# Holding a softmax's subtraction and exponential to their own step in the order of VectorE and ScalarE

## The chip, the cores and the metric

The kernel runs on one core of a Trainium2 chip. The metric is the device time of one execution in microseconds (us). PE is TensorE's matmul, PEld its weight load, DVE is VectorE, ACT is ScalarE, POOL is GpSimd and SP is the engine that issues most DMAs.

## The reference, cut to what matters

Two layers run over 1024 latent rows (16 batches of 64, width 128). Each layer attends from the latents to a context of 1601 rows and to the latents themselves, then goes through a scan and a feed-forward block. The attention takes nearly all of the time:

```python
q = ln @ Wq                                  # 16 heads of 64
k, v = split(concat([xn, ln]) @ Wkv)         # xn: normalized context
logits = einsum('bhld,bhsd->bhls', q * scale, k * scale)
w = softmax(logits)                          # layer 1: some context rows are masked
out = einsum('bhls,bhsd->bhld', w, v) @ Wo
x = x + out
x = x + scan_block(layernorm(x))             # after the attention, in each layer
x = x + ffn_block(layernorm(x))              # layer 0: experts; layer 1: 4-bit weights
```

## The kernel before, in words

The key weights are folded into the query and the value weights into the output, so that scores are made straight from the normalized context (`kvT`) and the averages are taken of the context itself (`kv`). A *group* is one layer, one batch and one half of the heads: 8 heads by 64 latents, or 512 columns. There are 64 groups. The context of a group is cut into 13 tiles of 128 rows, so a group has 13 *steps* and the whole has 832.

`step(n, ng)` writes the work of step n. The pieces that it calls belong to different groups, because the softmax has to know a group's maximum before it can weigh anything:

- `scores(g, i)`, L534: two matmul passes (L547) make a score tile `s` of 128x512 in PSUM, from a pool `pss` of three buffers. ACT copies it into the SBUF tile `st` (the "evict": L554 in layer 0, L552 in layer 1, where the mask is added). DVE takes the running maximum `R` (L561 or L559) from the same score tile. Two score tiles make a pair, one `st` tile of 128x1024; the thirteenth stands alone. A group has seven pairs, j = 0 to 6.
- `maximum(g)`, L564, one step after the group's last scores: transposes `tm` of R on PE and a reduction on DVE give the maximum `m`.
- `spread`, L584, two steps later: four matmuls (L588) write the maximum, spread over partitions, into a PSUM tile `mb`. It comes from the pool `pst` (tag `tp`) of three buffers that nearly all other small matmuls share, and lives until the group's last subtraction.
- `weigh(g, j)`, L591: DVE subtracts `mb` from the pair in place (L596), ACT takes the exponential in place (L597). It is written at the steps o = 3, 5, ..., 15 after the group's scores have ended.
- `average(g, i)`, L599, 21 steps behind the scores (`LAG`): matmuls (L609) with `st` as weights add the weighted context into a PSUM tile `av`, of which there is one (`psa`, two banks).
- `gather(g)`, L611: DVE takes the four parts out of `av` (L618) before the next group's averages can start.

Two further lists of generators are run beside the steps: `prep` (context, queries, latents of coming groups) and `between` (scans, experts, feed-forward blocks).

The order in which instructions stand on an engine is not the order of writing. A scheduler in the framework orders them by its own estimate of times, by the order of writing among those that are ready, and by any added edge. The kernel adds such edges with `behind(back)`, L1301. For the instructions that were written inside the block it looks up, for each engine, an instruction of the main pipeline in the list `self.place` (the score matmuls for PE, the evicts for ACT, the maxima for DVE), and lets none of them stand ahead of it. On PE this is always the latest score matmul; on ACT and DVE it is the latest for `back=0` and the one before it for `back=1`. The edge has no semaphore: it sets the order in the queue, and no wait at run time.

```python
for e, k in (("PE", 0), ("ACT", back), ("DVE", back)):
    if len(self.place[e]) > k:
        i = self.place[e][-1 - k]
        where[i.engine] = i
```

Of what is written in the steps, all but the scores, the averages, the gather and the weighing is already inside such a block.

Of the kernel before, what the change touches and what calls it, by code (L numbers as in the profile page):

```python
# [77 lines left out]
class Kernel:  # L78
# [1239 lines left out]
    def step(self, n, ng):  # L1318
        g, i = divmod(n, NT)
        if g < ng:  # L1320
            self.scores(g, i)

        ga, ia = divmod(n - LAG, NT)
        if 0 <= ga < ng and ia:
            if ia == 1:
                self.average(ga, 0)
            self.average(ga, ia)
            if ia == NT - 1:
                self.gather(ga)

        for p in (g - 2, g - 1):
            o = n - (p + 1) * NT
            if not 0 <= p < ng:
                continue
            if o == 1:
                with self.behind():
                    self.maximum(p)
            elif o == 3:
                with self.behind():
                    self.groups[p]["mb"] = self.spread(self.groups[p]["m"], f"mb{p}")  # L1340
            if o > 2 and o % 2 and (o - 3) // 2 < (NT + 1) // 2:
                self.weigh(p, (o - 3) // 2)

        d, o = divmod(n - LAG - NT, NT)
        if 0 <= d < ng:
            lay, b, half = self.groups[d]["key"]
            last = d == ng - 1
            with self.behind():
                if o == 0:
                    self.denominator(d)  # L1350
                elif o == (1 if last else 4):
                    self.turn(d)
                if last:
                    if o == 1:
                        self.output(lay, b // 2, 1)
                elif o == 7 and b % 2 and half:
                    self.output(lay, b // 2)
                elif o == 9 and d == ng - 2:
                    self.output(lay, b // 2, 0)
# [57 lines left out]
```

## Time and profile before

| | us |
|---|---|
| median of 3 runs | 2039.4 (2036.52 to 2041.78) |
| the profiled execution | 2037.05 |
| its span, first to last instruction | 2035.3 |
| PE busy | 1959.3 |
| PEld busy | 1486.4 |
| DVE busy | 1558.3 |
| ACT busy | 1405.2 |
| POOL busy | 512.0 |

The table is of one execution with the profiler. Engines run beside one another, so the busy times don't add up to the span. A matmul's end is modelled, and neighbouring matmuls overlap in the trace, so PE's busy time can hide short stalls. Where a row of the profile ends in an arrow, the engine sat idle before that work until the named work was done.

### The profile page before, as it was taken

The numbers are of one execution on the slowest core, as the hardware profiler recorded it, in microseconds if no ns is written. First come the engines' busy times: TensorE is split into PE (matmuls) and PEld (weight loads), VectorE is DVE, ScalarE is ACT, GpSimd is POOL, SyncE is SP. The second block draws the span as 40 slices with busy tenths as digits, with TensorE's granted clock in tenths as the row PEclk, the third lists the DMA queues.
The fourth block names the chain that finished last, engine by engine and source line by source line (L and its number), as shares of the span: only waits on it lengthen the run. The fifth ranks groups of instructions, "written<-read, shape, count | busy, mean of one in ns | idle before, by whom it ended". The sixth has DMA issues, their size and how long they took to land. (4 is left out here: it accounts for less than half of the span.)

```text
span 2035.3 us, 32662 instructions
## 1 busy us (share of the span) xinstructions
PE 1959.3 (96%) x12005; PEld 1486.4 (73%) x12005; DVE 1558.3 (77%) x2893; ACT 1405.2 (69%) x2673; POOL 512.0 (25%) x581
## 2 busy tenths in 40 slices
PE   7999999999999999999999999999999999999994
PEld 5677777676777766778777787777778777787783
DVE  4886667987777897776988777898686878778774
ACT  5787878888668887666767657776566656675651
POOL 3112113543113452121443203442111121101000
PEclk9999999999999999999999999999999999999996
DMA  5211112221122222221221102221120111101000
GB/s 143 69 60 52 52 52 73 82 66 50 35 76 86 66 76 57 64 74 47 67 80 50 36 24 71 75 59 51 43 56 15 57 36 47 46 1 36 23 1 21
DMA packets 142956, 110.53 MB, mean 54 GB/s; under 512 B 11458, under 2 KB 129486, under 8 KB 142798
## 3 DMA queue, kind: packets, MB, share of 16 engines
q1 hardware_dynamic: 140598, 107.40, 18.1%
q8 instruction: 95, 1.56, 0.3%
q10 hardware_dynamic: 2200, 1.06, 0.3%
q14 instruction: 63, 0.52, 0.1%
HBM read 79.97 MB, written 27.41 MB: 53 GB/s over the span
## 5 line engine op out<-in xcount | busy, mean ns | idle before, releaser
L609 PEld LDWEIGHTS av<-kv,st 128*128 128x128 f32 x6656 | 849.3, 192 | 310.1 <-issue 282.6
L609 PE MATMUL av<-kv,st 128*128 128x129 f32 x6656 | 866.1, 276 | 4.5 <-DVE aq L618 3.1
L547 PE MATMUL s<-qT,kvT 128*128 128x512 f32 x1664 | 848.5, 600 | 17.2 <-DVE R L561 14.5
L596 DVE TENSOR_TENSOR st<-st,mb 128x1024 f32<-128x1024 f32 (+1 forms) x448 | 502.5, 1135 | 1.2 <-PE mb L588 1.1
L597 ACT ACTIVATE st<-st 128x1024 f32<-128x1024 f32 (+1 forms) x448 | 445.5, 998 | 63.1 <-DVE st L596 59.5
L552 ACT ACTIVATE st<-s,mcol 128x512 f32<-128x512 f32 x416 | 283.8, 685 | 222.8 <-PE s L547 177.4
L554 ACT COPY st<-s 128x512 f32<-128x512 f32 x416 | 240.9, 583 | 125.9 <-PE s L547 99.0
L547 PEld LDWEIGHTS s<-qT,kvT 128*128 128x128 f32 x1664 | 258.9, 191 | 91.0 <-DVE R L561 40.2
L559 DVE SCALAR_TENSOR_TENSOR R<-s,mcol,R 128x512 f32<-128x512 f32 x352 | 262.9, 747 | 70.6 <-ACT st L552 69.6
L561 DVE TENSOR_TENSOR R<-s,R 128x512 f32<-128x512 f32 x352 | 241.6, 686 | 81.4 <-ACT st L554 79.6
L483 POOL TENSOR_TENSOR kv<-kv,vec 128x384 f32<-128x384 f32 (+1 forms) x128 | 135.9, 1081 | 155.4 <-PE kt L521 65.0
L628 POOL TENSOR_TENSOR aq<-aq,rd 128x512 f32<-128x512 f32 x63 | 77.0, 1222 | 359.2 <-DVE rd L625 351.9
L730 POOL TENSOR_TENSOR db<-sc_u,bb 128x512 f32<-128x512 f32 x64 | 84.8, 1327 | 134.8 <-DVE h L741 64.8
L747 POOL TENSOR_TENSOR sc_y<-sc_y,h 128x512 f32<-128x512 f32 x60 | 80.0, 1334 | 105.3 <-DVE h L746 81.3
L513 ACT ACTIVATE kv<-kv,coff,crstd 128x128 f32<-128x128 f32 x195 | 82.1, 494 | 8.2 <-POOL coff L510 8.2
L741 DVE TENSOR_TENSOR_SCAN h<-da,db 128x512 f32<-128x512 f32 x64 | 85.3, 1333 | 0.0
L504 ACT ACTIVATE scr<-kv,cmean 128x128 f32<-128x128 f32 x195 | 78.8, 404 | 6.9 <-DVE cmean L500 3.6
L561 DVE TENSOR_TENSOR R<-s,st 128x512 f32<-128x512 f32 x32 | 22.1, 690 | 78.4 <-ACT st L554 78.4
L618 DVE SCALAR_TENSOR_TENSOR aq<-xeb,ee,av 128x129 f32<-128x129 f32 x256 | 74.3, 346 | 3.4 <-PE av L609 3.4
L117 POOL TENSOR_TENSOR crstd<-cvar,neghalf 128x13 f32<-128x13 f32 x15 | 37.5, 2497 | 145.7 <-DVE cvar L508 145.5
L416 PE MATMUL q<-xnT,wqk 128*128 128x128 f32 x512 | 69.8, 281 | 0.0
L416 PEld LDWEIGHTS q<-xnT,wqk 128*128 128x128 f32 x512 | 64.4, 196 | 6.8 <-issue 3.3
(369 smaller groups left out, 1942.8 us busy)
## 6 DMA issues: line engine op xcount, KB each, us to landing
bb<-bcd SPq DMA_DIRECT2D x64, 256.0 KB, 4.4
xh<-kv SPq DMA_DIRECT2D x16, 832.0 KB, 4.8
kv<-xh SPq DMA_DIRECT2D x16, 832.0 KB, 5.4
kvT<-xhT SPq DMA_DIRECT2D x16, 800.0 KB, 4.5
xhT<-kvT SPq DMA_DIRECT2D x15, 800.0 KB, 3.5
kv<-in_ctx_dram SPq DMA_DIRECT2D x15, 768.0 KB, 5.2
ew<-in_e1T_dram SPq DMA_DIRECT2D x36, 64.0 KB, 1.8
ew<-in_e3T_dram SPq DMA_DIRECT2D x36, 64.0 KB, 1.9
```

Source lines behind the costliest of these rows:

```text
L416: nc.tensor.matmul(t[:, k * P:(k + 1) * P], self.wqk[:, g * 4 + k, :], xnT, start=True, stop=True)
L483: nc.gpsimd.tensor_tensor(kv[:, lo:hi, :D], kv[:, lo:hi, :D], self.row(self.vec[:, w1, :], [P, hi - lo, D]), ALU.mult)
L547: mm = nc.tensor.matmul(s, self.kv_of[lay, b][1][:, i * P:(i + 1) * P], q, start=True, stop=True)
L552: ev = nc.scalar.activation(st, s, AF.Identity, bias=mc)
L554: ev = nc.scalar.copy(st, s)
L559: mx = nc.vector.scalar_tensor_tensor(R, s, mc, last, ALU.add, ALU.max)
L561: mx = nc.vector.tensor_tensor(R, s, last, ALU.max)
L596: nc.vector.tensor_tensor(st, st, self.row(mb, [P, n, NQ]), ALU.subtract)
L597: nc.scalar.activation(st, st, AF.Exp)
L609: nc.tensor.matmul(o, st, self.kv_of[lay, b][0][:, i, :], start=(i == 0 and k % 2 == 0), stop=(i == NT - 1 and k % 2 == 1))
L730: nc.gpsimd.tensor_tensor(db, u, self.row(bb[:, 0, s % 2, :], both), ALU.mult)
L741: nc.vector.tensor_tensor_scan(flat(h), flat(da), flat(db), 0.0, ALU.mult, ALU.add)
```

## The change

The call of `weigh` in `step` is put into a block `behind(1)`. The subtraction of a pair may then not stand ahead of the last but one maximum written so far on DVE, nor its exponential ahead of the last but one evict on ACT. Nothing else is changed: same instructions, same buffers, same sizes. The edges act on the framework's ordering as a whole, so other instructions can change places too.

```diff
@@ -1339,7 +1339,8 @@
                 with self.behind():
                     self.groups[p]["mb"] = self.spread(self.groups[p]["m"], f"mb{p}")
             if o > 2 and o % 2 and (o - 3) // 2 < (NT + 1) // 2:
-                self.weigh(p, (o - 3) // 2)
+                with self.behind(1):
+                    self.weigh(p, (o - 3) // 2)
 
         d, o = divmod(n - LAG - NT, NT)
         if 0 <= d < ng:
```

## The prediction

> **What bounds the kernel now.** I read the page first, then the stages, then the waits, then one stretch in order of time. The page:
>
> ```profile
> span 2035.3 us, 32662 instructions
> PE 1959.3 (96%) x12005; PEld 1486.4 (73%) x12005; DVE 1558.3 (77%) x2893; ACT 1405.2 (69%) x2673; POOL 512.0 (25%) x581
> L596 DVE TENSOR_TENSOR st<-st,mb 128x1024 f32<-128x1024 f32 (+1 forms) x448 | 502.5, 1135 | 1.2 <-PE mb L588 1.1
> L597 ACT ACTIVATE st<-st 128x1024 f32<-128x1024 f32 (+1 forms) x448 | 445.5, 998 | 63.1 <-DVE st L596 59.5
> ```
>
> TensorE (PE) is the bound. The two rows below it are the work that the change holds: 448 subtractions on DVE and 448 exponentials on ACT. Each pair is 2.3 us of work, and a step of the pipeline (one score tile) lasts (1956-30)/832 = 2.31 us, from the first and last start of the score matmuls. The stages:
>
> ```profile
> 60.00:1960.00 1900.00, 1870.20 (x11505) 1416.73 (x11504) 1492.02 (x2710) 1352.03 (x2545) 483.82 (x516) 1.00 0.18 53
> 1960.00:2036.00 76.00, 44.02 (x296) 38.11 (x294) 38.73 (x102) 18.35 (x33) 5.49 (x12) 0.77 0.05 15
> ```
>
> The first column after the length is PE busy: idle 29.8 us in the body, 32 us in the tail. A change that moves only DVE and ACT work inside the body can win those 29.8 us, plus stalls that sit inside PE's modelled busy time, and no more. What PE waits for (us in total, times, longest):
>
> ```profile
> PEld s L547 <- DVE R L561: 40.2, 44, 2.5
> PEld s L547 <- DVE R L559: 18.4, 28, 1.5
> PE s L547 <- DVE R L561: 14.5, 17, 1.7
> PE s L547 <- DVE R L559: 2.2, 4, 0.7
> PEld av L609 <- ACT st L597: 6.1, 11, 2.4
> ```
>
> The score matmul waits for the running maximum R on DVE: R is the last reader of a score tile in PSUM, and there are three such buffers, so s of step i+3 waits for R of step i. The average's wait for the exponential is small. One stretch shows why R is late:
>
> ```profile
> 998.96 2.34 DVE L596 TENSOR_TENSOR st<-st,mb 128x1024 f32<-128x1024 f32 x2
> 1001.22 0.74 DVE L559 SCALAR_TENSOR_TENSOR R<-s,mcol,R 128x512 f32<-128x512 f32 x1
> 1001.88 1.21 DVE L596 TENSOR_TENSOR st<-st,mb 128x1024 f32<-128x1024 f32 x1
> ...
> 1004.26 1.21 DVE L596 TENSOR_TENSOR st<-st,mb 128x1024 f32<-128x1024 f32 x1
> 1005.39 0.75 DVE L559 SCALAR_TENSOR_TENSOR R<-s,mcol,R 128x512 f32<-128x512 f32 x1
> ...
> 1006.19 0.30 PEld L547 LDWEIGHTS s<-qT,kvT 128*128 128x128 f32 x2 [0.70 <-DVE R L559]
> 1007.11 0.30 PEld L547 LDWEIGHTS s<-qT,kvT 128*128 128x128 f32 x2 [0.62 <-DVE R L559]
> ```
>
> Four subtractions of a group come nearly together, DVE has no idle time from 1000 to 1012 (12.00 busy of 12.00), R falls behind, and three scores that PE runs back to back (while the previous group's sums are taken out of PSUM) find no free buffer.
>
> [...]
>
> **The change, part by part.** It adds no instruction and takes none away; the sum of busy times stays. It adds order only: the subtraction and exponential of pair j, at step o = 3+2j after their group's scores, must follow the maximum and the copy out of PSUM (evict) of the step before. I compared the built order of both programs. "Ahead of R_7" means the seventh maximum of the following group.
>
> - Subtractions: the median pair stood after R_3, 3, 4, 5, 8, 9, 10 (j = 0 to 6); now after R_3, 4, 6, 8, 10, 11, 14. Ahead of R_6 stood 3.52 per group, now 1.97; ahead of R_7 4.31, now 2.79. That is 1.5 x 1.21 = 1.85 us less DVE work in front of just those maxima that the back-to-back scores s_9 and s_10 wait for. Two or more subtractions between neighbouring maxima: 79 places, now 1.
> - Exponentials: ahead of evict 7 stood 2.97 per group, now 1.97: 1.06 us less ACT work ahead of it, and R waits for the evict.
> - What it is worth. The exposed s-waits: the PE rows are stall in full (14.5 + 2.2 = 16.7 us). Of the PEld rows most is hidden, because a weight load has a running matmul to hide behind: in the stretch, two waits of 1.32 us cost PE 0.19 us (three scores took 1008.07 - 1005.29 = 2.78 us; one takes 0.86, as from 1000.04 to 1000.90 where nothing waits, so 2.59 unhindered). At that share 58.6 us are 8 us. Sum 25 us. Were all of them gone: -25. The waits are 0.8 us each (58.6+16.7 over 93), below the 1.85 us that is taken out, but DVE also works on scans (1.22 and 0.68 us) and the taking-out (4 x 0.35), so that it stays behind in part. I take 60%: -15 us. Ends: 0 and -25.
> - What is late next. The subtractions go to steps 8 to 14, where DVE had about 1.5 fewer. Worked out from the starts and ends in the trace, the room between R of step i and s of step i+3 is, in the median, 3.3 us or more for i = 9 to 12, against 1.0 and 0.5 us for i = 6 and 7. A subtraction of 1.21 us fits. Some of the later R will slip; I take +2 us, between 0 and +8 (10 of 62 groups at 0.8 us).
> - Exponential before average: the median time from exponential to the average that reads it is between 10 and 17 us for each j. The exponentials move later by 0 to 3 steps in the median, at most 7 us; 3 us or more stay in the median, so no wait is added as a rule. The average's order on PE hardly moves (3154 of 3328 matmuls stand between the same scores, 152 earlier, 22 later). Cost 0, up to +6 (a doubling of the 6.1 us).
> - ACT: an exponential now stands closer to its subtraction, and what is queued behind it is the next evict. "ACT st <- DVE st" is 59.5 us in 88 waits now, 0.68 each; ACT is 69% busy. I take +1, between 0 and +10.
> - SP and POOL: same work, a few neighbours exchanged; POOL waits on the maxima's engine anyway and is 25% busy. DMA is at 0.18 share. Zero, hidden behind PE.
> - Tail: the last group's subtractions have the same neighbours as before. The last one of the group before moves behind the last maximum, which ends at 1958.0; the next DVE work on the chain starts at 1960.10 after 2.08 us of idle, and 0.68 us fits. Zero.
>
> Sum: -15 + 2 + 0 + 1 = -12 us against the profiled execution, 2037.05 us (span 2035.3 and 1.75 around it): 2025. The median of the runs, 2039.4, is 2.4 above that execution, so 2027.
>
> **Rivals.**
>
> 1. *Scores stay as late* (no change). The subtractions fill the same queue, only later: the late maxima become R_9 to R_12 and the gain is given back. For it: DVE at 77% has no slack in stretches with a scan beside. Against it: the 3.3 us of room there. Time: -15 + 15 = 0, so 2039, between 2034 and 2045.
> 2. *The stall disappears entirely*: -25, and the "issue" idle and the rest of 29.8 us shrink with it: down to 2011.
> 3. *Slower: the broadcast maxima hold their PSUM bank longer.* mb (L588) sits in one of three shared tp buffers from its first matmul to the seventh subtraction: 18.5 us in the mean, worked out from the trace, of a group's 30. With that subtraction after R_14 instead of R_10 it is 9 us longer, nearly always alive; queries, transposes, projections and routing then have two buffers. They fill about 1250 us of buffer time in all, 0.6 of a buffer on average. Taken as random, two or more are then wanted at once in 13% of the time; in 64 x 9 = 576 us that is 75 us; when PE waits through a third of it, +25, against the -12: 2052. It decides when the built order puts a query or transpose at the head of PE's queue while both are taken. For it: 48 of 256 query matmuls and 48 of 180 transposes of the context stand one or two scores later. Against it: they were moved out of the way, so PE has other work in front.
> 4. *The added order doesn't bind* is excluded by the built order: 327 of 448 subtractions stand elsewhere.
>
> **How the numbers follow.** About 0.3% (6 us) is what a measurement of this kernel can tell from no change. Forecast and rival 2 together 0.70 (2011 to 2033), rival 1 0.17, rival 3 0.13. Predicted time: 2027. The range takes in the unknown costs of the forecast (-25 to about 0) and rival 1 up to 2044; below 2011 nothing is left to win by these terms, and 2052 is left out. Own range of the forecast: 2012 to 2033. Chances: faster 0.70, same 0.17, slower 0.13.
>
> **What would show it.** In the profile of the changed kernel: "s <- DVE R" falls from 75.3 us on PE and PEld to 30 or less; PE idle from 60 to 1960 us falls from 29.8 to about 18; no pair of subtractions in one piece of DVE's time order; "av <- ACT st L597" stays under 15 us; busy times of DVE and ACT within 1%. Wrong, if "s <- DVE R" falls and the span doesn't (then look at tp: waits of q, kt, tm or at on ACT or DVE), or if it doesn't fall (rival 1).

## The result, and the profile after

The changed kernel is slower, by about 18 us. Its median is 2058.72 us (2055.5 to 2060.7) against 2040.59 us (2036.52 to 2044.27) before, four runs each: ratio 1.0084, 95% interval 1.0063 to 1.0105. A second set of runs, labelled e14, gave 1.0083 (1.0065 to 1.0101):

> The changed kernel itself beside these two: slower than before by 14 to 20 us.

The forecast was 2027 us, in a range up to 2044.

First the page of the changed kernel, the same rows as before: busy us, share and count of each engine, then two rows of groups (busy us and mean ns of one, then the idle time ahead of it and what ended it).

```profile
span 2059.0 us, 32649 instructions
PE 1974.0 (96%) x12005; PEld 1493.5 (73%) x12005; DVE 1561.0 (76%) x2893; ACT 1410.8 (69%) x2673; POOL 508.5 (25%) x581
...
L597 ACT ACTIVATE st<-st 128x1024 f32<-128x1024 f32 (+1 forms) x448 | 445.1, 994 | 127.1 <-DVE st L596 125.0
L596 DVE TENSOR_TENSOR st<-st,mb 128x1024 f32<-128x1024 f32 (+1 forms) x448 | 506.8, 1132 | 4.8 <-PE mb L588 4.6
```

Neither of the two held operations takes longer: 994 and 1132 ns in the mean, before 998 and 1135. Beside PE's busy time only one number in these rows has moved far: the idle time that ACT spends in front of an exponential because its subtraction isn't done. It went from 59.5 to 125.0 us. Next the stages of the changed kernel (window in us, its length, then busy us of PE, PEld, DVE, ACT, POOL; granted clock, DMA share, GB/s).

```profile
60.00:1984.00 1924.00, 1885.77 (x11532) 1423.96 (x11531) 1498.68 (x2719) 1359.91 (x2552) 481.83 (x518) 1.00 0.18 52
1984.00:2060.00 76.00, 43.70 (x293) 37.85 (x292) 38.53 (x102) 18.31 (x33) 5.50 (x12) 0.77 0.05 15
```

The tail is as before (idle 32.3 us, before 32.0). The body is 24 us longer. PE idle in it is 1924.00 - 1885.77 = 38.2 us, before 29.8, which makes 8.4 us. PE's busy time there grew by 15.6 us. About 6.8 us of that go back to periods in which the clock was granted at half: ahead of the tail there are 17.1 us of them in this execution and 3.4 us in the profiled one of before, and half of such a period is taken as lost: the two matmuls of a score start 0.85 us apart in them and 0.43 us elsewhere. The longest, 10.2 us, lies at 49 us, ahead of the body. It puts the scores back by 5 us, so that 27 more matmuls fall into the body (x11532 against x11505). The other 8.8 us are, by this estimate, stalls inside busy time, which a modelled end of a matmul hides. So 8.4 + 8.8 = 17 us come from the change. The starts of the score matmuls agree: from the first to the last they take 23.4 us longer, and less 6.8 us this is 16.6 us. The waits of the changed kernel (us in total, times, longest):

```profile
DVE R L561 <- ACT st L554: 163.5, 141, 7.6
...
ACT st L597 <- DVE st L596: 125.0, 160, 3.4
DVE R L559 <- ACT st L552: 112.7, 105, 4.4
...
PEld s L547 <- DVE R L561: 36.7, 42, 2.7
...
PEld s L547 <- DVE R L559: 19.8, 24, 2.0
...
PE s L547 <- DVE R L561: 14.6, 23, 1.9
...
PEld av L609 <- ACT st L597: 9.6, 16, 2.4
...
PE s L547 <- DVE R L559: 5.4, 6, 1.2
```

The score's waits for R, which were to fall from 75.3 us to 30, are 76.5 us. ACT waits for 160 subtractions, before for 88. One stretch of the changed kernel shows what such a wait is tied to; first DVE in order of time (start, length, engine, line, operation; a bracket is idle time before it and what ended it).

```profile
1014.99 1.21 DVE L596 TENSOR_TENSOR st<-st,mb 128x1024 f32<-128x1024 f32 x1
1016.11 0.74 DVE L559 SCALAR_TENSOR_TENSOR R<-s,mcol,R 128x512 f32<-128x512 f32 x1
1016.77 1.21 DVE L596 TENSOR_TENSOR st<-st,mb 128x1024 f32<-128x1024 f32 x1
1017.90 0.74 DVE L559 SCALAR_TENSOR_TENSOR R<-s,mcol,R 128x512 f32<-128x512 f32 x1
1018.57 0.68 DVE L746 TENSOR_TENSOR h<-h,bb 128x512 f32<-128x512 f32 x1
1019.69 0.75 DVE L559 SCALAR_TENSOR_TENSOR R<-s,mcol,R 128x512 f32<-128x512 f32 x1 [0.44 <-ACT st L552]
1020.36 1.21 DVE L596 TENSOR_TENSOR st<-st,mb 128x1024 f32<-128x1024 f32 x1
```

The same stretch on ACT:

```profile
1016.23 1.06 ACT L597 ACTIVATE st<-st 128x1024 f32<-128x1024 f32 x1 [1.92 <-DVE st L596]
1017.19 0.67 ACT L552 ACTIVATE st<-s,mcol 128x512 f32<-128x512 f32 x1
1018.02 1.06 ACT L597 ACTIVATE st<-st 128x1024 f32<-128x1024 f32 x1 [0.15 <-DVE st L596]
1018.98 0.67 ACT L552 ACTIVATE st<-s,mcol 128x512 f32<-128x512 f32 x1
...
1021.60 1.06 ACT L597 ACTIVATE st<-st 128x1024 f32<-128x1024 f32 x1 [0.57 <-DVE st L596]
```

And on the weight loads and matmuls of the scores:

```profile
1020.49 0.30 PEld L547 LDWEIGHTS s<-qT,kvT 128*128 128x128 f32 x2 [0.79 <-DVE R L559]
1022.28 0.30 PEld L547 LDWEIGHTS s<-qT,kvT 128*128 128x128 f32 x2 [1.49 <-DVE R L559]
...
1014.25 1.02 PE L547 MATMUL s<-qT,kvT 128*128 128x512 f32 x2
...
1016.00 1.02 PE L547 MATMUL s<-qT,kvT 128*128 128x512 f32 x2
...
1017.76 1.02 PE L547 MATMUL s<-qT,kvT 128*128 128x512 f32 x2
...
1022.28 1.12 PE L547 MATMUL s<-qT,kvT 128*128 128x512 f32 x2 [0.66 <-DVE R L559]
```

Follow one chain. A subtraction ends on DVE at 1017.98, the exponential starts at 1018.02. The evict of a score tile stands behind it on ACT and starts at 1018.98. R needs that evict (in this trace and in that of before, each of the 768 R starts at least 31 ns after the end of its tile's evict): DVE, which has nothing else to do, waits 0.44 us for ACT and runs R at 1019.69 (the scan block's operation at 1018.57 was over by then). The next held subtraction stands behind R, at 1020.36, and the next exponential behind that, at 1021.60. Meanwhile the scores on PE wait for R. Subtraction, exponential, evict, maximum and subtraction again follow one another over two engines, and on both the operations run one behind another (from 1014 to 1023 us none starts more than 0.11 us before the end of the one ahead of it); from 1016.77 to 1020.36 one turn took 3.59 us, about the 3.50 us that PE needs for two steps of scores and averages here (score matmuls at 1014.25, 1016.00, 1017.76). A turn serves two steps, so here it has no slack to make up any delay. Whether this chain is the cost is for the experiments to say.

### The profile page after: what moved, and what is told of

Same layout as the page of the kernel before. It is cut to its first block, busy times and chain, and to the rows that moved or that the text cites. A ratio compares the mean times of both kernels' runs of the same rounds, so it can differ in the third digit from the quotient of the medians.

```text
span 2059.0 us, 32649 instructions
## 1 busy us (share of the span) xinstructions
PE 1974.0 (96%) x12005; PEld 1493.5 (73%) x12005; DVE 1561.0 (76%) x2893; ACT 1410.8 (69%) x2673; POOL 508.5 (25%) x581
## 3 DMA queue, kind: packets, MB, share of 16 engines
q10 hardware_dynamic: 2200, 1.06, 0.3%
## 5 line engine op out<-in xcount | busy, mean ns | idle before, releaser
L597 ACT ACTIVATE st<-st 128x1024 f32<-128x1024 f32 (+1 forms) x448 | 445.1, 994 | 127.1 <-DVE st L596 125.0
L596 DVE TENSOR_TENSOR st<-st,mb 128x1024 f32<-128x1024 f32 (+1 forms) x448 | 506.8, 1132 | 4.8 <-PE mb L588 4.6
L628 POOL TENSOR_TENSOR aq<-aq,rd 128x512 f32<-128x512 f32 x63 | 71.3, 1132 | 326.2 <-DVE rd L625 316.3
L747 POOL TENSOR_TENSOR sc_y<-sc_y,h 128x512 f32<-128x512 f32 x60 | 84.7, 1412 | 117.9 <-DVE h L746 104.4
L416 PEld LDWEIGHTS q<-xnT,wqk 128*128 128x128 f32 x512 | 64.9, 195 | 11.7 <-issue 3.5
L416 PE MATMUL q<-xnT,wqk 128*128 128x128 f32 x512 | 70.5, 281 | 0.1
```

What stands on the lines that cost most here:

```text
L416: nc.tensor.matmul(t[:, k * P:(k + 1) * P], self.wqk[:, g * 4 + k, :], xnT, start=True, stop=True)
L596: nc.vector.tensor_tensor(st, st, self.row(mb, [P, n, NQ]), ALU.subtract)
L597: nc.scalar.activation(st, st, AF.Exp)
L747: nc.gpsimd.tensor_tensor(y, y, h, ALU.add)
```

## The experiments

All ratios below are to the kernel before in the same set of runs, with the 95% interval. "ACT's wait" is the total that exponentials (or the operation named) wait for their subtraction; "s-waits" are all waits of the scores for R, 75.3 us before and 76.5 after.

### Is it the PSUM bank of the broadcast maxima?

In the changed kernel `mb` lives 27.1 us in the mean, before 18.5. e1 is the kernel before with one small read of `mb` at the step of the changed kernel's last subtraction, so that the bank is held as long and nothing else is moved.

```diff
+            if o == 15:
+                with self.behind(1):
+                    self.nc.vector.tensor_copy(self.sm([P, 1], "hold"), self.groups[p]["mb"][:, :1])
```

> The kernel before with one thing added: a copy of one column (128x1) of the broadcast maxima mb into SBUF at step o = 15, behind the last but one maximum. It keeps mb's PSUM buffer occupied as long as in the changed kernel (about 27 us a group instead of 18.5) while every subtraction and exponential stays where it was before; 64 copies of some 0.1 us on DVE. Bank theory (the longer hold of the shared PSUM buffer is the loss): slower than before by 10 to 18 us. Queue theory (exponentials stand right behind their subtractions, and the copies out of PSUM behind them are held up on ACT) and crowding theory (subtractions moved into steps 11 to 15 delay the maxima there): within 4 us of before.

Measured: 2043.35 us, 1.0006 (0.9995 to 1.0016). `mb` lived 26.35 us. The bank was held, and it cost nothing.

e2 and e3 go the other way. `mb` is copied into SBUF and its bank is free at once, in the kernel before (e2) and in the changed one (e3).

```diff
-                    self.groups[p]["mb"] = self.spread(self.groups[p]["m"], f"mb{p}")
+                    t = self.spread(self.groups[p]["m"], f"mb{p}")
+                    mb = self.groups[p]["mb"] = self.at.tile([P, NQ], F32, tag="mbs", name=f"mbs{p}", bufs=2)
+                    self.nc.vector.tensor_copy(mb, t)
```

> The kernel before, with mb copied by DVE from PSUM to SBUF (128x512, about 0.65 us, 64 times) as soon as it is made, and the subtractions reading the copy; the PSUM buffer is free after the copy. It is the control of the next kernel. All theories: between 10 us faster and 15 us slower than before; the 42 us of added DVE work lie in front of the first subtraction of a group, where PE has other work.

> The changed kernel with the same copy of mb to SBUF: the shared PSUM buffer is given back at once although the subtractions are held. Bank theory: no slower than the control without the hold (within 4 us), for the hold no longer occupies a bank. Queue and crowding theories: slower than that control by 10 to 18 us, as the changed kernel is than before.

Measured: e2 2104.62 us, 1.0306 (1.0282 to 1.0330), far outside what was expected; e3 2126.48 us, 1.0409 (1.0387 to 1.0431). The copy itself was dear (last section). But with the bank free in both, the change still costs 2126.48 - 2104.62 = 21.9 us. Freeing the bank takes none of the loss away. Rival 3 is out.

### Which half of the held pair costs?

e4 holds the exponentials only; the subtractions stand wherever the scheduler puts them. e5 holds the subtractions as the change does, and writes the exponential of a pair two steps later.

```diff
# e4                       (behind gets an own number for DVE; 1 << 20 holds nothing)
-                self.weigh(p, (o - 3) // 2)
+                with self.behind(1, 1 << 20):
+                    self.weigh(p, (o - 3) // 2)
# e5                       (weigh without its exponential, which is raise_e)
+                with self.behind(1):
+                    self.weigh(p, (o - 3) // 2)
+            if o > 4 and o % 2 and (o - 5) // 2 < (NT + 1) // 2:
+                with self.behind(1):
+                    self.raise_e(p, (o - 5) // 2)
```

> Only the exponentials are held (behind the last but one copy out of PSUM on ACT); the subtractions stand as early as before, so mb is given back as before, and 265 of 434 exponentials stand two steps or more behind their subtraction (79 are such in the changed kernel... 86 with those of three). Bank and crowding theories: within 5 us of before. Queue theory: as fast as before or faster, ACT's wait for the subtraction falls from 59.5 us to under 30. If holding the exponentials itself is the loss (averages that wait for them): slower by 10 us or more.

> The changed kernel, with the exponential written two steps after its subtraction (held behind the last but one copy out of PSUM of that later step). The subtractions stand as in the changed kernel; an exponential then follows its subtraction by 2.1 steps in the mean instead of 1.1, so ACT should hardly wait for a subtraction (125 us in the changed kernel). Queue theory (the ACT queue, and the copies out of PSUM in it, stand still for a subtraction that is late): back to within 6 us of before. Crowding theory (the moved subtractions delay the maxima of the late steps on DVE): slower than before by 12 to 24 us, as the changed kernel.

Measured: e4 2044.48 us, 1.0002 (0.9989 to 1.0014), ACT's wait 41.2 us in 56 places (less than 30 us were expected). e5 2044.59 us, 1.0011 (1.0001 to 1.0020). Both are as fast as the kernel before, within 0.2%. In e5 421 of the 448 subtractions stand behind the same maximum as in the changed kernel, by the order in the traces, so their late places on DVE are not the loss. Neither half alone costs more than these 0.2%; the two together cost 18 us. One thing the two runs share: their exponentials stand further from the subtractions, two steps or more in 265 (e4) and 351 (e5) of 434 cases, against 86 in the changed kernel. A kernel with early subtractions and exponentials right behind them was not run. e5's waits, with the exponential on a line of its own (L601):

```profile
PEld s L547 <- DVE R L561: 26.5, 29, 2.8
...
ACT st L601 <- DVE st L596: 23.4, 29, 2.6
...
PEld s L547 <- DVE R L559: 12.5, 16, 2.1
...
PE s L547 <- DVE R L561: 10.9, 15, 1.9
...
PE s L547 <- DVE R L559: 2.7, 6, 1.3
```

and e5's body, with the columns of the stages above:

```profile
60.00:1966.00 1906.00, 1878.63 (x11538) 1425.11 (x11537) 1489.62 (x2716) 1353.17 (x2547) 482.15 (x516) 1.00 0.18 52
```

ACT's wait is 23.4 us, below that of before. The s-waits fell to 52.6 us: the step that the forecast had hoped for, a good part of it. And PE's idle time in the body is 1906.00 - 1878.63 = 27.4 us, against 29.8: 22.7 us less of this wait went with 2.4 us less of idle, and no time was won.

Two relatives of e5 leave the subtractions free (e9) or hold them behind the last but three maxima (e10), with the exponentials as in e5:

```diff
# e9
                 self.weigh(p, (o - 3) // 2)
# e10
+                with self.behind(3):
+                    self.weigh(p, (o - 3) // 2)
```

> The subtractions free as in the kernel before (mean places 3.1 to 10.5), the exponentials written two steps after them and held as in e5: 3.4 steps in the mean between the two instead of 1.6 before. Queue theory: ACT's wait for subtractions falls below e5's 23 us, and the score matmul's wait for R with it; 0 to 8 us faster than before. If e5 came back to before only because the held subtractions bring a gain that the queue eats up, this kernel lacks that gain: within 2 us of before.

> The subtractions held two places more loosely than in the change (mean places 3.1, 3.5, 4.6, 6.5, 8.9, 10.1, 11.6), the exponentials as in e5 and e9. The wait on ACT is gone and the burst of subtractions is partly spread: the version that should beat before if anything of my forecast holds, by 3 to 10 us. If spreading the subtractions is worth nothing: as e9.

Measured: 2043.78 us, 1.0003 (0.9989 to 1.0016), and 2043.85 us, 1.0005 (0.9992 to 1.0019), with ACT's wait at 11.5 and 12.8 us. The gains that were expected, up to 8 us in e9 and 3 to 10 us in e10, did not come: nothing is won below the time before by taking more of ACT's wait away either.

### How far, and which pairs?

e6 holds only the pairs j = 4 to 6, e7 only j = 0 to 3; e8 holds all of them one step less strictly, `behind(2)`, and e11 one step more, `behind(0)`. e17 writes the exponential one step after the held subtraction, half of the way to e5.

```diff
# e6 (e7: j < 4)
+                if j >= 4:
+                    with self.behind(1):
+                        self.weigh(p, j)
+                else:
+                    self.weigh(p, j)
# e17
+            if o > 3 and o % 2 == 0 and (o - 4) // 2 < (NT + 1) // 2:
+                with self.behind(1):
+                    self.raise_e(p, (o - 4) // 2)
```

> Only the pairs j = 4 to 6 are held, j = 0 to 3 stand as before. Mean step of the subtractions ahead of which maximum they stand: 3.1, 3.5, 4.5, 6.0, 10.1, 11.3, 14.2 (before: 3.1, 3.4, 4.4, 5.6, 7.8, 9.2, 10.5). Crowding theory: nearly the whole loss, 12 to 18 us. Queue theory: in proportion to the pairs, some 8 us. If the loss goes by how far the subtractions are put off in all (8.7 of 13.6 steps a group): 11 us.

> Only the pairs j = 0 to 3 are held; the mean places are 3.1, 4.2, 6.2, 8.3, 9.6, 10.5, 11.5. Crowding theory in the late steps: within 5 us of before. Queue theory: 10 us slower. By how far the subtractions are put off in all (9.4 of 13.6 steps a group): 12 us slower. My own forecast had a gain here, since these are the subtractions ahead of the maxima 4 to 7: -15 to -5 us.

> The change with a hold that is one step looser: behind the maximum, or copy, two before the last but one is now the third last. Mean places 3.1, 3.5, 5.3, 8.0, 9.5, 10.7, 12.3. By how far the subtractions are put off (8.4 of 13.6 steps): 11 us slower than before. Queue theory (exponentials follow by 1.3 steps, as in the changed kernel): 12 to 18 us. Crowding in steps 11 to 14 only: under 6 us.

> The hold one step tighter than in the change: behind the last maximum and the last copy out of PSUM (mean places 3.1, 5.1, 7.0, 9, 11, 12, 15; exponentials 1.2 steps behind, as in the change). Queue theory: the same closeness, at a later place; as the changed kernel or somewhat slower, 14 to 28 us slower than before, with 110 us or more of ACT's wait for subtractions. If the loss went by how far subtractions are put off (18.1 steps a group against 13.6): 24 us.

> The change with the exponential written one step after its subtraction: 131 of 434 stand two steps or more behind it (86 in the change, 351 in e5). Loop theory: a part of the loss is gone, 6 to 15 us slower than before. If only a full two steps of distance help: as the change, 16 to 18 us.

| | us | ratio (95%) | ACT's wait, us (times) |
|---|---|---|---|
| e6, late pairs | 2060.32 | 1.0079 (1.0059 to 1.0098) | 91.0 (127) |
| e7, early pairs | 2054.11 | 1.0049 (1.0032 to 1.0067) | 98.8 (126) |
| e8, two back | 2055.49 | 1.0064 (1.0044 to 1.0084) | 93.2 (112) |
| e11, none back | 2067.90 | 1.0123 (1.0097 to 1.0149) | 101.5 (131) |
| e17, exponential one later | 2058.49 | 1.0069 (1.0046 to 1.0091) | 107.1 (126) |

Each of these costs time, and each has 91 us or more of ACT's wait, where the runs above that cost nothing (e1, e4, e5, e9, e10) have 60 or less. But the wait is no measure of the loss: e11 has less of it than the change (125.0 us; 110 or more were expected of e11) and loses more, and holding the late pairs alone (e6) and the early pairs alone (e7) loses 0.79% and 0.49%, together more than the 0.84% of the whole. One step of distance for the exponential (e17) is not enough, two (e5) are.

### Is the wait itself the price?

e12 puts a wait back into e5: a copy of one column of the pair, on ACT, where the change has its exponential. e13 has the same copy of a constant column, which waits for nothing. e15 and e16 do the same with a copy of 512 columns.

```diff
# e5, and inside the block of weigh:
# e12
+                    self.nc.scalar.copy(self.sm([P, 1], "probe"), self.groups[p]["st"][(o - 3) // 2][:, 0, :1])
# e13
+                    self.nc.scalar.copy(self.sm([P, 1], "probe"), self.ident[:, :1])
# e15 (e16: the same size, from the constant wqk)
+                    self.nc.scalar.copy(self.at.tile([P, NQ], F32, tag="probe", name="probe", bufs=1), self.groups[p]["st"][(o - 3) // 2][:, 0, :])
```

> e5 with a small ACT copy (128x1, some 0.2 us) of the pair's first column right after each subtraction, held where the change holds the exponential; the exponential itself stays two steps later. The copy waits for the subtraction, so ACT's queue stands still for it as in the change, without the exponential's length. Queue theory: ACT's wait for subtractions comes back to 90 us or more and the kernel is 10 to 20 us slower than e13. If the place of the exponential's own length was the matter: within 4 us of e13.

> The control of e12: the same 448 small ACT copies at the same place in the program, but of a column of a constant tile, so they wait for nothing. Some 90 us of ACT work added to an engine that is 69% busy. Both theories: within 6 us of e5, so 0 to 8 us slower than before.

> As e12, with a copy of half the pair (128x512, some 0.6 us) instead of one column behind the late subtraction; it waits for it. Loop theory (in the change a maximum 0.69, a subtraction 1.21, an exponential 1.06 and a copy out of PSUM 0.58 us follow one another across DVE and ACT, 3.5 us and the hand-overs, about two steps of 1.75): the op of 0.6 us makes it 3.1 us, so some of the loss comes back, 3 to 12 us more than e16. If neither wait nor length matters: within 3 us of e16.

> The control of e15: the same copy of 128x512 at the same place, from a tile of folded weights, so without a wait for the subtraction. 448 x 0.6 = 270 us more on ACT, which then is 82% busy. All theories: slower than e5 by 0 to 20 us through ACT's load alone.

The group of the copy in e12 (busy us, mean ns | idle before it, releaser):

```profile
L1348 ACT COPY probe<-st 128x1 f32<-128x1 f32 x448 | 84.4, 188 | 93.3 <-DVE st L596 90.9
```

in e15:

```profile
L1348 ACT COPY probe<-st 128x512 f32<-128x512 f32 x448 | 276.7, 618 | 74.6 <-DVE st L596 72.6
```

and in e16:

```profile
L1348 ACT COPY probe<-wqk 128x512 f32<-128x512 f32 x448 | 277.0, 618 | 1.5 <-DVE wqk L318 1.4
```

| | copy | waits for the subtraction | us | ratio (95%) |
|---|---|---|---|---|
| e13 | 188 ns | no | 2046.88 | 1.0019 (1.0010 to 1.0029) |
| e12 | 188 ns | yes, 90.9 us | 2043.95 | 1.0003 (0.9992 to 1.0013) |
| e16 | 618 ns | no | 2059.17 | 1.0075 (1.0052 to 1.0097) |
| e15 | 618 ns | yes, 72.6 us | 2075.36 | 1.0150 (1.0126 to 1.0175) |

With a short copy 90.9 us of waiting cost nothing (2.9 us less than without it), where the queue theory had expected 10 to 20 us. With a longer one 72.6 us of waiting cost 16.2 us more than the same copy without a wait, above the 3 to 12 us that were expected. So ACT standing still in front of a late subtraction isn't the price by itself. In e15 a longer operation follows that wait, ahead of what is queued behind it, and there it is dear. One reservation: e15 and e16 also load ACT more, 78% busy against 69%, and the load alone costs (e16 against e13, 12.3 us), so that length behind a wait and a fuller ACT aren't told apart by these four.

A count over the whole traces, worked out from their starts and ends, points the same way. Take each evict that stood on ACT behind an operation that had waited for a subtraction, with no pause between them, and whose score matmuls were done before that operation was. Add up how long after the end of its score matmuls each of these evicts started. That is 65 us in the kernel before and 150 us in the changed one; 7 to 64 us in e1, e4, e5, e9 and e10, which cost nothing; 90 to 135 us in e6, e7, e8, e11 and e17, which cost time. e12 has 63 us and e15 82 us, their controls 27 and 18 us. So, e16 and its load apart, this count parts the runs with a loss from those without. But it doesn't give the size: e11, which loses most of the five, has 110 us.

## Why the prediction was wrong

**The failed step is the term for ACT.** The prediction gave "an exponential now stands closer to its subtraction, and what is queued behind it is the next evict" +1 us, between 0 and +10. The wait it named did what it said, 59.5 to 125.0 us, but the upper end of the term was too low: with the exponentials out of the way (e5) nearly the same order of DVE costs 2.2 us (0.2 to 4.1), with them at the subtraction's heels it costs 18 us, so that they make some 16 us. With 16 in place of 1 the forecast's own sum would have been 3 us slower, not 12 faster. The term was weighed as 0.68 us of wait here and there on an engine with 31% to spare. What stands behind the exponential is an evict of 0.67 us that R waits for, and R is what both the score and the next held subtraction wait for. That the wait closes a loop with R was not seen.

**The gain of -15 us was not there either.** It had two parts, and both failed.
- R of steps 6 and 7 was to come 1.85 us earlier. Measured from the start of the step's score to the end of R, R of i = 4 to 7 took 3.53, 3.77, 3.95 and 3.74 us before and 3.32, 3.62, 3.59 and 3.57 us after: 0.15 to 0.36 us earlier (means of 61 groups). Fewer subtractions stood in front, as forecast from the order. But R also needs the evict of its own tile, and that hardly moved: it ended 1.96, 2.43, 2.46 and 2.27 us after the start of the score before, and 2.02, 2.37, 2.38 and 2.22 us after it in the changed kernel. In these four steps the evict was the last thing that R waited for in 91 of 244 cases, before in 32. Over all steps R's wait for the evict did not grow: it is 163.5 + 112.7 = 276.2 us in the two layers, 158.0 + 122.1 = 280.1 us before. Where the exponentials are moved away as well, in e5, these four times of R are 3.06, 3.28, 3.20 and 3.26 us.
- The waits of the scores were priced at 25 us of lost time for 75.3 us of wait, a third. e5 took 22.7 us of them away: 3.1 us of the PE rows and 19.6 us of the PEld rows, at the prediction's prices (in full, and a seventh) 6 us. PE's idle time fell by 2.4 us and the time didn't fall at all. What took the place of these waits was not followed; how much of the 25 us is to be had at all, no run here showed.

**Late crowding, +2 us,** was right in direction and small: R of i = 11, 12, 1, 2, 3 comes 0.2 to 0.45 us later than before. In e5, with the subtractions at nearly the same places, these R are at most 0.14 us later than before, and the kernel is no more than 2 us slower. So most of the lateness came with the exponentials, and crowding on DVE by itself costs next to nothing.

**Right were** the zero for the tail, "av <- ACT st" (9.6 us, under 15), busy times within 1%, and the 27 us that `mb` now lives. Rival 3 started from that life and came nearest in time, 2052 us, by a mechanism that e1 and e3 rule out: the bank was held, and that cost nothing. Of the prediction's tests, the last one spoke plainly: "s <- DVE R" didn't fall, which by its own words pointed to rival 1, no change. Its list of signs had no case in which both the waits stay and the time grows.

**What is shown and what is argued.** Shown: with the subtractions held, the loss needs their exponentials close behind them (e5), and holding the exponentials alone doesn't bring it (e4); it is neither the bank, nor late work on DVE, nor ACT's idle time as such (e1, e3, e5, e12). Shown with the reservation above: after a wait, the length of what follows it counts (e15 against e16). The count of evicts that are held up goes with the loss, but that alone doesn't prove it to be the cause. Argued from one stretch: that the loop of subtraction, exponential, evict and maximum, at 3.59 us for two steps of 3.50 us, is how the lateness persists. It agrees with e4 (no late subtraction), e5 (no exponential in the loop), e12 (0.19 us in the loop in place of 1.06) and e15. Open: how the delay reaches PE. Of the 16.5 us that matmul starts lie further apart (half-clock time counted at half, and each gap put to the matmul that ends it), some 4.5 are at the scores, 3.4 at the output's transposes (L639; their weight loads wait 3.5 us for POOL, in three places, and their matmuls 2.9 us, in two), 3.2 at the queries (L416), and the rest is spread thinly, with lines that won time among it. And no run explains why the losses of e6 and e7 don't add up to that of the change.

## What to carry to other kernels

Before holding an instruction in an engine's order, read what stands behind it and behind its consumer in the order of every engine concerned: the consumer here, 1.06 us long, waited for the held producer ahead of the evicts on which the next step depends. In this kernel a producer could be held without loss only together with room for its consumer: two steps of distance for the exponential took the loss away, to within 2 us. And price a wait by taking it away or putting it in, not by its total: 22.7 us less of one wait was worth nothing on the bounding engine, 90.9 us more of another cost nothing, and 72.6 us of that same wait ahead of a longer operation, on a fuller ACT, cost 16 us.

## What the runs showed of the hardware

**Half-clock periods of TensorE.** The traces of the two kernels have stretches ahead of the tail in which PE's clock was granted at half: of 10.2 us at 49 us, 3.4 at 509 and 3.4 at 1673 in the profiled execution of the changed kernel, one of 3.4 us at 403 before. In the 3.4 us ahead of these four periods PE was busy for 69%, 24% and 60% of the time in the changed kernel and 49% before, and its longest single gap there was 2.6 us. Other windows as thin (27% from 493.4 to 496.8 us before, 30% from 1303.0 to 1306.4 in the changed kernel, both at full clock) were not followed by half clock, so what decides is open. Over 98 executions of the kernel before, the time follows the mean granted clock, 16.6 us for each 0.01 (0.991 to 0.984, 2035.7 to 2049.4 us). At equal clock the change still costs 15 to 16 us.

**With `mb` in SBUF, the subtraction and POOL's work took longer.** e2's copy of `mb` was to cost up to 15 us and cost 62. Two groups of the kernel before, shapes kept apart:

```profile
L596 DVE TENSOR_TENSOR st<-st,mb 128x1024 f32<-128x1024 f32 x384 | 460.0, 1211 | 1.2 <-PE mb L588 1.1
...
L730 POOL TENSOR_TENSOR db<-sc_u,bb 128x512 f32<-128x512 f32 x64 | 84.8, 1327 | 134.8 <-DVE h L741 64.8 <-DMA bb<-bcd 22.9 <-DVE sc_u L714 18.8
```

and of e2:

```profile
L596 DVE TENSOR_TENSOR st<-st,mbs 128x1024 f32<-128x1024 f32 x384 | 498.5, 1305 | 1.2
...
L730 POOL TENSOR_TENSOR db<-sc_u,bb 128x512 f32<-128x512 f32 x64 | 107.2, 1678 | 126.6 <-DVE h L741 73.0 <-DMA bb<-bcd 20.0 <-DVE sc_u L714 17.5
```

The subtraction takes 1305 ns in place of 1211 with `mb` in PSUM, and the operation on POOL 1678 ns in place of 1327; POOL is busy for 600.5 us from 60 to 1960 us, against 483.8 before. The subtraction's extra time lies where POOL is at work: in e2's trace the 194 subtractions during which no POOL operation ran took 1218 ns in the mean, the 190 others 1394 ns; with `mb` in PSUM POOL made no such difference (1214 and 1209 ns). What links them was not shown. The longer subtractions, (1305 - 1211) x 384 = 36 us for a pair and (817 - 675) x 64 = 9 us for the single tile, and 64 copies of 682 ns, 44 us, are 89 us more on DVE; how that becomes 62 us of time was not followed further.
